# Low halves of q and k taken straight from PSUM, normalization on GpSimd, and new layouts for stored q, k and v

## The chip, the cores and the metric

The kernel runs on one core of a Trainium2 chip. The metric is the device time of one execution in microseconds, as the median of several runs. The engines are named as in the profile: PE (TensorE), DVE (VectorE), ACT (ScalarE), POOL (GpSimd) and SP (SyncE, whose queue issues every DMA of this kernel).

## The reference

The input x has 16 sequences of 512 rows with 128 features. Each row is normalized once (`_layernorm`), and two branches read the result:

```python
mu = jnp.mean(x, axis=-1, keepdims=True); var = jnp.var(x, axis=-1, keepdims=True)
xn = (x - mu) / jnp.sqrt(var + 1e-05) * ln_g + ln_b          # a second time, in the attention branch
q, k, v = xn @ Wq + bq, xn @ Wk + bk, xn @ Wv + bv            # 16 heads of 8 features
content = jnp.einsum('bihd,bjhd->bhij', q + u_bias, k)
pos = _relative_shift(jnp.einsum('bihd,jhd->bhij', q + v_bias, p))   # p = pe @ Wp
attn = softmax((content + pos) * scale); out = (attn @ v) @ Wo + bo
```

The other branch is a feed-forward net with weights of +1 and -1: `[x, -x] @ k0` (512 wide), relu, `@ k1` (512), relu, `@ k2` (128), with three scale factors. The output is the sum of x and both branches.

## The kernel before

The program has two stages. The first one prepares, batch by batch (b = 0 to 15), everything that attention reads, and computes the feed-forward net beside it. The second one is attention, head by head.

**Halves.** TensorE is fast with f16 operands, so a 32-bit value t is given as two f16 values, hi = f16(t) and lo = f16(t - hi), and products of halves are added. So q + u, q + v, k and the positions p each exist as a hi and a lo half. A power of two as a scale (`q_mul`, `k_mul`, found in `powers` at run time) keeps them within f16's range; `e_scale` undoes it at the exponential.

**The first stage.** `norm` (L308) computes mean and variance on DVE (L318, L319), a refined inverse root by a chain of 8-element operations (L325 to L333), and then writes xn in place with four 128x128 operations (L335). `transposed2` (L505) transposes xn on PE and writes its halves for the feed-forward net, and `with_bias` (L518) writes x2T, the input of the projections. `project_q` (L543) multiplies with `wq_d`; ACT reads the product twice with scale and bias (`scaled`, L522, line L528), once for q + u and once for q + v, into 32-bit tiles in SBUF; `halves_to` (L501) then casts the tile to hi on ACT (L502) and subtracts on POOL for lo (L503). `project_k` (L563) does the same once, through `stored` (L533). `project_v` copies v with ACT. All are stored to DRAM scratch tensors with DMAs: `qu_scr` (a zero-interleaved pair of columns for each value, four parts), `k_scr` (four parts, each half twice), `v_scr` and, after all batches, `qv_scr` (`quads_stored`, L599).

The feed-forward net runs between: for each batch four products of layer 0 (2 matmuls each, L640), four of layer 1 (8 matmuls each, L640), and the last layer (32 matmuls, L674). A product of layer 0 or 1 is split in halves by ACT and DVE (`split`, L617 and L618) before the next layer reads it. Its result is added to the residual, which POOL prepares (`ffn_residual`, L662) and DVE finishes (`ffn_out`, L688).

**PSUM.** Six tiles `s_t` of one bank, `t_t` and `a_t` are in use. The feed-forward products rotate over four banks (`F_BANKS`, L190), and everything else that goes through `psw` (L235) over three.

**Order.** In the first stage the program's text gives priorities (the list `queue` and the function `more`, L749, put the items of the attention preparation between the feed-forward products; `SPAN` = 12.3 batches is how far they are spread) and a scheduler decides the order on each engine. An engine works through its instructions in order; so does SP's queue, where a DMA that waits holds those behind it. In attention the order of PE, DVE and ACT is written out by hand (`STEPS`, L41), and SP and POOL are left to the scheduler.

**Attention.** A unit is four rows of queries of all 16 batches for one head; there are 512 units. `scores` (L785) adds the products of k and the two position windows in PSUM (L797, L813, L826), DVE finds maxima (L840, L845, L854), PE subtracts them (L859), ACT exponentiates (L869), PE multiplies with v (L887). At the second unit of each group of eight, `load_queries` (L210) issues the 12 DMAs of the next group's queries, into the one of two tiles that was used before; once a head, `load_head` (L196) issues the next head's k, windows and v. Once a head as well, `divided` (L939) loads sums and their reciprocals, multiplies them on POOL (L946) and stores them (L947).

Of the kernel before, what the change touches and what calls it, by code (L numbers as in the profile page):

```python
# [9 lines left out]
F32 = mybir.dt.float32  # L10
F32R = mybir.dt.float32r
F16 = mybir.dt.float16
# [3 lines left out]
AF = mybir.ActivationFunctionType  # L16
# [71 lines left out]
def rel_attention_and_binary_ffn(  # L88
# [47 lines left out]
    def scr(name, shape, dt):  # L136
# [3 lines left out]

    qu_scr = scr("qu_scr", [4, DH * H, B, S, 2], F16)
    qv_scr = scr("qv_scr", [4, DH * H, 5, NL, NC, UL, B], F16)
    k_scr = scr("k_scr", [4, DH * H, B, S], F16)
    p_scr = scr("p_scr", [4, DH * H, 2, WIN + 4], F16)
    pd_scr = scr("pd_scr", [4, DH * H, 2, 2, WIND + 1], F16)
    v_scr = scr("v_scr", [P, H, B, NC * VW], F32)

# [3 lines left out]
    res_scr = scr("res_scr", [B, S, D], F32)  # L151
    Q_PARTS, K_PARTS = ((0, 2), (1, 3)), ((0, 1), (2, 3))

# [26 lines left out]

    s_t = [
        [ps.tile([P, 2, NC, 4, B], F32, tag=f"s_{n}_{m}", name=f"s_{n}_{m}") for m in range(2)]
        for n in range(3)
    ]
    t_t = ps.tile([P, 4, 2, P], BF16, tag="t", name="t_t")
# [3 lines left out]
    p_banks.append(t_t.rearrange("p n f i -> p (n f i)").bitcast(F32))  # L189
    F_BANKS = (3, 4, 5, 6)  # L190
    t_bank = p_banks[6].rearrange("p (g i) -> p g i", g=2)
# [4 lines left out]
    def load_head(h):  # L196
        m = h % 2
        src = p_scr.rearrange("t (d h) s j -> (t d) h s j", h=H)[:, h]
        src_d = pd_scr.rearrange("t (d h) s n j -> (t d) h s n j", h=H)[:, h]
        for n in range(4):  # L200
            rows_n = slice(32 * n, 32 * n + 32)
            nc.sync.dma_start(
                k_t[m][rows_n], k_scr.rearrange("t (d h) b j -> (t d) h b j", h=H)[:, h, n::4, :]
            )
            nc.sync.dma_start(win[m][rows_n], src[:, :, 3 - n : 3 - n + WIN])
            r, side = n // 2, n % 2
            nc.sync.dma_start(win_d[m][rows_n], src_d[:, side, :, 1 - r : 1 - r + WIND])
        nc.sync.dma_start(v_t[m], v_scr[:, h].rearrange("p b f -> p (b f)"))

    def load_queries(h, l):  # L210
        m = l % 2
        qv = qv_scr.rearrange("t (d h) r l a u b -> (t d) h r l (a u b)", h=H)[:, h, :, l]
        qu = qu_scr.rearrange("t (d h) b i m -> (t d) h b (i m)", h=H)[:, h]
        for n in range(4):
            rows_n = slice(32 * n, 32 * n + 32)
            nc.sync.dma_start(
                qc_t[m][rows_n, :, n // 2].rearrange("p g i m -> p g (i m)"),
                qu[:, n::4, 2 * l * P : 2 * (l + 1) * P],
            )
            nc.sync.dma_start(  # L220
                qp_t[m][rows_n, :, n].rearrange("p s a u b -> p s (a u b)"), qv[:, n : n + 2]
            )
            r, side = n // 2, n % 2
            nc.sync.dma_start(
                qd_t[m][rows_n, :, r].rearrange("p t a u b -> p t (a u b)"),
                qv[:, r + side : r + side + 3 : 2],
            )


    with ExitStack() as pre:  # L230
# [19 lines left out]
        xn_all = {}  # L250
        XB = 4
        RB = 3
# [55 lines left out]
        def norm(b):  # L308
# [25 lines left out]
            for c in range(NC):  # L334
                nc.vector.tensor_scalar(  # L335
                    xn[:, c, :], xn[:, c, :], st1[:, b, c, 0:1], r[:, 1, c : c + 1], ALU.subtract, ALU.mult
                )
# [66 lines left out]
        pw = sts("pw", [P, 2])  # L404
        k_mul = pw[:, 1:2]
        q_mul = sts("q_mul", [P, 1])
        b_cols = sts("b_cols", [P, 3])
# [14 lines left out]
        def powers():  # L422
# [24 lines left out]
            nc.vector.tensor_scalar(e_scale, e_scale, 2.0 ** -26, None, ALU.mult)  # L447
            for n in range(2):
# [6 lines left out]
        def positions():  # L455
            pp = psw("pp")
            nc.tensor.matmul(pp, lhsT=wp_d, rhs=pe_sb, start=True, stop=True)
            p32 = work.tile([P, S], F32, tag="t32", name="p32", bufs=2)
            nc.scalar.activation(p32, pp, AF.Identity, scale=k_mul)
            halves_to(p32, *[t[:, PAD : PAD + S] for t in p_half])  # L460

        def windows():
            for n in range(2):
                for part in K_PARTS[n]:
# [20 lines left out]
        def clear():  # L485
            for t in v_b:
                nc.gpsimd.memset(t, 1.0)
            for t in p_half:
                nc.gpsimd.memset(t, 0.0)
            for ts in qu_b:  # L490
                for t in ts:
                    nc.gpsimd.memset(t, 0.0)

# [6 lines left out]

        def halves_to(src, hi, lo):  # L501
            nc.scalar.copy(hi, src)  # L502
            return nc.gpsimd.tensor_tensor(lo, src, hi, ALU.subtract)  # L503

# [16 lines left out]

        def scaled(b, n, src, dst):  # L522

            mul = k_mul if n == 2 else q_mul
            if n < 2:
                src = src.rearrange("p (a l m) -> p l a m", a=NC, l=NL)
                dst = dst.rearrange("p (l a m) -> p l a m", l=NL, a=NC)
            nc.scalar.activation(dst, src, AF.Identity, bias=b_cols[:, n : n + 1], scale=mul)  # L528

        def t32(b, n):  # L530
            return work.tile([P, S], F32, tag="t32", name=f"t32_{b}_{n}", bufs=2)

        def stored(b, t, dst, parts):  # L533
            hv = [work.tile([P, S], F16, tag=f"hv{m}", name=f"hv{m}_{b}", bufs=2) for m in range(2)]
            last = halves_to(t, *hv)
            for m in range(2):
                for part in parts[m]:
                    nc.sync.dma_start(dst[part, :, b, :], hv[m])
            return last

        two = {}

        def project_q(b):  # L543
            pq = psw(f"pq_{b}")
            nc.tensor.matmul(pq, lhsT=wq_d, rhs=x2T[b], start=True, stop=True)
            n = b % 2

            if n == 0:
                two[0] = work.tile([P, S, 2], F32, tag="two", name=f"two_{b}", bufs=1)
            tu = t32(b, 0)  # L550
            scaled(b, 0, pq, tu)
            scaled(b, 1, pq, two[0][:, :, n])
            halves_to(tu, *[t[:, :, n] for t in qu_b[n]])
# [3 lines left out]
            if n == 1:  # L557
                halves_to(
                    two[0].rearrange("p (q r) n -> p r q n", r=4),
                    *[q[:, :, :, b - 1 : b + 1] for q in qv_all],  # L560
                )

        def project_k(b):  # L563
            pk = psw(f"pk_{b}")
            nc.tensor.matmul(pk, lhsT=wk_d, rhs=x2T[b], start=True, stop=True)
            t = t32(b, 2)
            scaled(b, 2, pk, t)
            last = stored(b, t, k_scr, K_PARTS)
            with tc.issue_after(last.ins):
                clear_queries(b)  # L570

        def project_v(b):
# [13 lines left out]
            )  # L586
            nc.sync.dma_start(v_scr[:, :, b, :], vb.rearrange("p h c w -> p h (c w)"))

# [69 lines left out]
        def ffn_residual(b):  # L658
            res = last_res if b == LAST else spare[:, 4 + b % (RB + 1)]
            rows_of = res.rearrange("p (c d) -> p c d", c=NC)  # L660
            nc.sync.dma_start(rows_of, x[b].rearrange("(c p) d -> p c d", p=P))
            nc.gpsimd.tensor_tensor(rows_of, rows_of, bo_sb.unsqueeze(1).to_broadcast([P, NC, D]), ALU.add)  # L662
            acts[b, 3] = res
# [70 lines left out]
        for b in range(B):  # L734
            queue.append(lambda b=b: project_q(b))
            if b + 3 < B:
# [410 lines left out]
```

## Time and profile before

| what | value |
|---|---|
| median of 3 runs | 1378.01 us (1374.29 to 1380.7) |
| profiled execution, its own time | 1373.51 us |
| its span, first to last instruction | 1371.7 us |
| granted TensorE clock, mean | 0.985 |
| busy: PE, DVE, ACT, POOL | 1295.0, 1137.7, 832.6, 130.8 us |
| first attention matmul | 266.5 us after the span's start |
| DMA bytes | 160.22 MB, mean 117 GB/s |

How to read it: all times are microseconds unless ns is written. A row of a table of stretches gives busy time of the engines in a stretch of the span, with the number of instructions; a row of a timeline gives the start, the duration, the engine, the line of the program, the operation, and output <- input, with the idle time before it and what ended that in brackets. A row of waits gives who waited for whom: us in total, times, longest.

### The profile page before, as it was taken

What the parts mean: (1) busy time and instruction counts of PE and PEld (TensorE: products, weight loads), DVE (VectorE), ACT (ScalarE), POOL (GpSimd) and SP (SyncE); (2) the same over time, 40 slices, a digit from 0 to 9 for tenths busy, and PEclk for the clock granted to TensorE, in tenths of its full rate; (3) what the DMA queues carried; (4) which work ended last, traced back from release to release, by engine and by line L of the source; (5) the groups of instructions that cost most, each with busy time, mean ns of one, the idle gap of its engine ahead of it and who ended that gap; (6) DMA issues with size and microseconds to landing.
All of it is one profiled execution on the core that took longest, in us unless ns stands there. A gap on an engine that the chain in (4) does not pass through costs nothing. (4 is left out here: it accounts for less than half of the span.)

```text
span 1371.7 us, 55178 instructions
## 1 busy us (share of the span) xinstructions
PE 1295.0 (94%) x23061; PEld 970.3 (71%) x23061; DVE 1137.7 (83%) x2723; ACT 832.6 (61%) x1456; POOL 130.8 (10%) x115
## 2 busy tenths in 40 slices
PE   4988889999999999999999999999999999999966
PEld 2555555577778777777877877778777777777744
DVE  8988754688888888888888888888888888888846
ACT  4566668466666666666666666666666666566630
POOL 4333345010000000000000000000000000000011
PEclk9999999999999999999999999999999999999988
DMA  4587869873232333333333323333333253323288
GB/s 117 171 222 192 191 171 257 242 220 92 76 99 74 94 79 95 95 86 86 93 89 83 94 74 97 83 93 84 95 80 99 75 128 84 95 74 88 68 146 190
DMA packets 243606, 160.22 MB, mean 117 GB/s; under 512 B 79510, under 2 KB 227100, under 8 KB 243356
## 3 DMA queue, kind: packets, MB, share of 16 engines
q1 hardware_dynamic: 243356, 156.69, 43.5%
q8 instruction: 181, 2.97, 0.9%
q14 instruction: 69, 0.57, 0.1%
HBM read 96.34 MB, written 59.48 MB: 114 GB/s over the span
## 5 line engine op out<-in xcount | busy, mean ns | idle before, releaser
L869 ACT ACTIVATE e<-s,e_scale 128x512 f32<-128x512 f32 x1024 | 623.7, 690 | 218.2 <-PE s L859 218.1
L845 DVE TENSOR_TENSOR m<-s,m 128x256 bf16<-128x256 f32 x1024 | 431.6, 422 | 112.9 <-PE s L826 77.6
L797 PE MATMUL s<-q,k 128*128 128x64 f16 x8192 | 406.7, 193 | 2.1 <-issue 1.0
L859 PE MATMUL s<-ident_b,nm 128*128 128x256 bf16 x2048 | 383.8, 275 | 7.3 <-DVE nm L854 7.3
L797 PEld LDWEIGHTS <-k 128*128 128x128 f16 x8192 | 358.5, 98 | 23.6 <-issue 2.8
L840 DVE TENSOR_REDUCE m<-s 128x256 bf16<-128x512 f32 x512 | 348.2, 680 | 1.0 <-ACT e L869 0.6
L813 PE MATMUL s<-q,win 128*128 128x128 f16 (+1 forms) x4096 | 342.8, 206 | 0.1
L887 PE MATMUL a_t<-e,v 128*9 128x256 f32 x4032 | 266.0, 381 | 0.6 <-ACT e L869 0.6
L813 PEld LDWEIGHTS <-win 128*128 128x128 f16 x4096 | 231.4, 98 | 0.3 <-issue 0.3
L826 PE MATMUL s<-q,win_d 128*128 128x64 f16 x2048 | 227.7, 193 | 0.0
L854 DVE TENSOR_REDUCE nm<-t_t 128x2 bf16<-128x256 bf16 x512 | 214.7, 419 | 7.1 <-PE t_t L850 2.9
L859 PEld LDWEIGHTS <-nm 128*128 128x128 bf16 x2048 | 131.0, 98 | 117.8 <-DVE m L845 99.0
L896 ACT COPY av<-a_t 128x256 f32<-128x256 f32 x126 | 46.9, 372 | 186.2 <-PE a_t L887 161.2
L887 PEld LDWEIGHTS a_t<-e,v 128*9 128x9 f32 x4032 | 86.4, 90 | 81.2 <-issue 1.6
L850 PE MATMUL t_t<-ident_b,m 128*128 128x128 bf16 x1024 | 141.3, 220 | 1.4 <-DVE m L845 1.3
L826 PEld LDWEIGHTS <-win_d 128*128 128x128 f16 x2048 | 129.8, 98 | 0.0
L946 POOL TENSOR_TENSOR raw<-raw,rden 128x512 f32<-128x512 f32 x15 | 19.1, 1273 | 992.3 <-DMA rden<-rden_scr 992.3
L640 PEld LDWEIGHTS <-e 128*128 128x128 f16 x512 | 49.6, 98 | 59.7 <-issue 12.6
L850 PEld LDWEIGHTS <-m 128*128 128x128 bf16 x1024 | 80.9, 98 | 11.3 <-DVE m L845 4.9
L618 DVE SCALAR_TENSOR_TENSOR h2l<-s,h2h 128x512 f16<-128x512 f32 x45 | 30.9, 686 | 37.6 <-ACT h2h L617 37.4
L640 PE MATMUL s<-h1l,e 128*128 128x512 f16 x180 | 47.2, 379 | 0.5 <-DVE h1l L618 0.4
L640 PE MATMUL s<-h1h,e 128*128 128x512 f16 x180 | 47.2, 384 | 0.3 <-DVE h1l L618 0.2
(176 smaller groups left out, 888.3 us busy)
## 6 DMA issues: line engine op xcount, KB each, us to landing
q<-qv_scr SPq DMA_DIRECT2D x512, 64.0 KB
q<-qu_scr SPq DMA_DIRECT2D x256, 64.0 KB
qu_scr<-k SPq DMA_DIRECT2D x32, 256.0 KB
k_scr<-hv SPq DMA_DIRECT2D x64, 128.0 KB
qu_scr<-win SPq DMA_DIRECT2D x32, 256.0 KB
qv_scr<-e SPq DMA_DIRECT2D x16, 512.0 KB
k<-k_scr SPq DMA_DIRECT2D x64, 128.0 KB
win<-p_scr SPq DMA_DIRECT2D x64, 79.5 KB
```

The source lines that it names most:

```text
L640: nc.tensor.matmul(ph, lhsT=w[:, t, f * P : (f + 1) * P], rhs=h[t][m], start=(m == 0 and t == 0), stop=(m == 1 and t == n - 1),)
L797: nc.tensor.matmul(sp[:, c % 2, :, :, 4 * g : 4 * g + 4].rearrange("p a r (n m) -> p n (a r) m", m=2), lhsT=kt[:, g, c * P : (c + 1) * P], ...
L813: nc.tensor.matmul(blocks[:, x0 : x0 + (NC + 1) * (len(cs) - 1) + 1 : NC + 1], lhsT=win[h % 2][:, side, y0 : y0 + P], rhs=qp[:, side, :, c ...
L826: nc.tensor.matmul(blocks[:, x0 : x0 + NC + 2 : NC + 1, 2 * t : 2 * t + 2], lhsT=win_d[h % 2][:, t, UP_OFF - 4 * u : WIND - 4 * u], rhs=qd ...
L840: nc.vector.tensor_reduce(st["m"], flat(st["ps"][0]).rearrange("p c x -> p x c"), AX.X, ALU.max)
L845: nc.vector.tensor_tensor(st["m"], flat(st["ps"][1])[:, c], st["m"], ALU.max)
L850: nc.tensor.transpose(st["pt"][:, f, :], st["m"][:, f * P : (f + 1) * P], ident_b)
L854: nc.vector.tensor_reduce(st["nm"], st["pt"], AX.X, ALU.max, negate=True)
L859: nc.tensor.matmul(flat(st["ps"][half])[:, :, f * P : (f + 1) * P], lhsT=st["nm"][:, f : f + 1].to_broadcast([P, P]), rhs=ident_b.unsqueez ...
L869: nc.scalar.activation(st["eT"][:, :, cs, :, i0 : i0 + 4].rearrange("p b c a r -> p (c a) b r"), st["ps"][half].rearrange("p c a r b -> p ...
L887: nc.tensor.matmul(bank[32 * r : 32 * r + VW, g], lhsT=v_t[h % 2][:, v0 : v0 + VW], rhs=pair["eT"][:, b, c], start=(c == 0 and (g == 0 or ...
L896: nc.scalar.copy(pair[half][:, g], bank[:, g])
```

## The change

- `halves_to` takes the product in PSUM itself: ACT writes hi with the bias, and DVE (no longer POOL) computes lo = (product + bias) - hi in one operation. The scale is no longer applied there; instead the weights `wp_d`, `wq_d` and `wk_d` are multiplied by `q_mul` or `k_mul` once, in `powers`. The 32-bit tiles in SBUF and `scaled` are gone.
- q is projected for two batches at once, into a pair of banks of its own. The two batches of a pair now stand side by side in `qu_scr`, in place of one batch and zeros, so it is half as large. `load_queries` loads both columns and then clears the other batch's column with a POOL memset, four for each group.
- `k_scr` has two parts instead of four, and `load_head` loads each twice. `v_scr` has batch ahead of head: the store is one piece for each partition, and the load of a head takes 16 pieces.
- The four 128x128 operations of `norm` move from DVE to POOL.
- The feed-forward net has three banks instead of four, the rest of `psw` two instead of three. Six x tiles are kept instead of four. `clear_queries` moves from behind the k halves to behind the residual. The clearing of the staging tiles of q + u goes.

```diff
-    qu_scr = scr("qu_scr", [4, DH * H, B, S, 2], F16)
+    qu_scr = scr("qu_scr", [4, DH * H, B // 2, S, 2], F16)
-    k_scr = scr("k_scr", [4, DH * H, B, S], F16)
+    k_scr = scr("k_scr", [2, DH * H, B, S], F16)
-    v_scr = scr("v_scr", [P, H, B, NC * VW], F32)
+    v_scr = scr("v_scr", [P, B, H, NC * VW], F32)
-    Q_PARTS, K_PARTS = ((0, 2), (1, 3)), ((0, 1), (2, 3))
+    Q_PARTS, P_PARTS, K_PARTS = ((0, 3), (1, 2)), ((0, 2), (1, 3)), ((0,), (1,))
...
-    F_BANKS = (3, 4, 5, 6)
+    F_BANKS = (4, 5, 6)
+    q_banks = s_two[0].rearrange("p m c a r b -> p m (c a r b)")
...
-            nc.sync.dma_start(
-                k_t[m][rows_n], k_scr.rearrange("t (d h) b j -> (t d) h b j", h=H)[:, h, n::4, :]
-            )
+            for x in range(2):
+                nc.sync.dma_start(
+                    k_t[m][32 * n + 16 * x : 32 * n + 16 * x + 16],
+                    k_scr.rearrange("t (d h) b j -> (t d) h b j", h=H)[:, h, n::4, :],
+                )
...
-                qu[:, n::4, 2 * l * P : 2 * (l + 1) * P],
-            )
+                qu[:, n // 2 :: 2, 2 * l * P : 2 * (l + 1) * P],
+            )
+            nc.gpsimd.memset(qc_t[m][rows_n, :, n // 2, :, 1 - n % 2], 0.0)
...
-        def psw(name, banks=(0, 1, 2)):
+        def psw(name, banks=(2, 3)):
...
-        XB = 4
+        XB = 6
...
             for c in range(NC):
-                nc.vector.tensor_scalar(
+                nc.gpsimd.tensor_scalar(
                     xn[:, c, :], xn[:, c, :], st1[:, b, c, 0:1], r[:, 1, c : c + 1], ALU.subtract, ALU.mult
                 )
...
-            nc.vector.tensor_scalar(q_mul, pw[:, 0:1], scale, None, ALU.mult)
+            for t, mul in ((wp_d, k_mul), (wq_d, q_mul), (wk_d, k_mul)):
+                nc.vector.tensor_scalar(t, t, mul, None, ALU.mult)
...
-        def halves_to(src, hi, lo):
-            nc.scalar.copy(hi, src)
-            return nc.gpsimd.tensor_tensor(lo, src, hi, ALU.subtract)
+        def halves_to(src, n, hi, lo):
+            nc.scalar.activation(hi, src, AF.Identity, bias=b_cols[:, n : n + 1])
+            for r in range(4) if len(src.shape) == 4 else [slice(None)]:
+                nc.vector.scalar_tensor_tensor(
+                    lo[:, r], src[:, r], b_cols[:, n : n + 1], hi[:, r], ALU.add, ALU.subtract
+                )
...
         def project_q(b):
+            for n in range(2):
+                nc.tensor.matmul(
+                    q_banks[:, n],
+                    lhsT=wq_d,
+                    rhs=x2T[b + n].rearrange("p (a l m) -> p l a m", a=NC, l=NL),
+                    start=True,
+                    stop=True,
+                )
+            qu = qu_b[b // 2 % 2]
+            halves_to(q_banks.rearrange("p n j -> p j n"), 0, *qu)
             for m in range(2):
                 for part in Q_PARTS[m]:
-                    nc.sync.dma_start(qu_scr[part, :, b], qu_b[n][m])
+                    nc.sync.dma_start(qu_scr[part, :, b // 2], qu[m])
+            halves_to(
+                q_banks.rearrange("p n (q r) -> p r q n", r=4), 1, *[q[:, :, :, b : b + 2] for q in qv_all]
+            )
...
-            nc.sync.dma_start(v_scr[:, :, b, :], vb.rearrange("p h c w -> p h (c w)"))
+            nc.sync.dma_start(v_scr[:, b], vb.rearrange("p h c w -> p h (c w)"))
...
         for b in range(B):
-            queue.append(lambda b=b: project_q(b))
+            if b % 2:
+                queue.append(lambda b=b: project_q(b - 1))
```

More of the change, by code (lines that the diff above doesn't have):

```diff
@@ L179, in rel_attention_and_binary_ffn @@
     a_t = ps.tile([P, 2, 2 * P], F32, tag="a", name="a_t")
[L181 to L184, printed above, removed]
+    s_two = [ps.tile([P, 2, 2, NC, 4, B], F32, tag=f"s_{n}", name=f"s_{n}") for n in range(3)]
+    s_t = [[t[:, m] for m in range(2)] for t in s_two]
     t_t = ps.tile([P, 4, 2, P], BF16, tag="t", name="t_t")
@@ L207, in load_head @@
             nc.sync.dma_start(win_d[m][rows_n], src_d[:, side, :, 1 - r : 1 - r + WIND])
-        nc.sync.dma_start(v_t[m], v_scr[:, h].rearrange("p b f -> p (b f)"))
+        nc.sync.dma_start(v_t[m].rearrange("p (b f) -> p b f", b=B), v_scr[:, :, h])
     def load_queries(h, l):
@@ L404, in rel_attention_and_binary_ffn @@
         pw = sts("pw", [P, 2])
-        k_mul = pw[:, 1:2]
-        q_mul = sts("q_mul", [P, 1])
+        q_mul, k_mul = pw[:, 0:1], pw[:, 1:2]
         b_cols = sts("b_cols", [P, 3])
@@ L444, in powers @@
             nc.vector.tensor_scalar(pw, pw, 2.0 ** 13, None, ALU.mult)
-            nc.vector.tensor_scalar(q_mul, pw[:, 0:1], scale, None, ALU.mult)
+            for t, mul in ((wp_d, k_mul), (wq_d, q_mul), (wk_d, k_mul)):
+                nc.vector.tensor_scalar(t, t, mul, None, ALU.mult)
             nc.vector.tensor_tensor(e_scale, bmax[:, 0:1], bmax[:, 1:2], ALU.mult)
-            nc.vector.tensor_scalar(e_scale, e_scale, 2.0 ** -26, None, ALU.mult)
+            nc.vector.tensor_scalar(e_scale, e_scale, 2.0 ** -26 * scale, None, ALU.mult)
             for n in range(2):
@@ L457, in positions @@
             nc.tensor.matmul(pp, lhsT=wp_d, rhs=pe_sb, start=True, stop=True)
-            p32 = work.tile([P, S], F32, tag="t32", name="p32", bufs=2)
-            nc.scalar.activation(p32, pp, AF.Identity, scale=k_mul)
-            halves_to(p32, *[t[:, PAD : PAD + S] for t in p_half])
+            hi, lo = [t[:, PAD : PAD + S] for t in p_half]
+            nc.scalar.copy(hi, pp)
+            nc.vector.tensor_tensor(lo, pp, hi, ALU.subtract)
         def windows():
             for n in range(2):
-                for part in K_PARTS[n]:
+                for part in P_PARTS[n]:
                     for side, x0, d0 in ((0, PAD, PAD + S - P + 2), (1, 0, PAD - P + 1)):
@@ L489, in clear @@
                 nc.gpsimd.memset(t, 0.0)
-            for ts in qu_b:
-                for t in ts:
-                    nc.gpsimd.memset(t, 0.0)
         def clear_queries(b):
@@ L520, in with_bias @@
             nc.scalar.activation(x2T[b], flipped.pop(b), AF.Identity, bias=b_c, scale=g_c)
[L522 to L541, printed above, removed]
-        def project_q(b):
[L544 to L553, printed above, removed]
+        def project_q(b):
+            for n in range(2):
[8 more added lines that the diff above has]
+            halves_to(q_banks.rearrange("p n j -> p j n"), 0, *qu)
             for m in range(2):
                 for part in Q_PARTS[m]:
-                    nc.sync.dma_start(qu_scr[part, :, b], qu_b[n][m])
[L557 to L560, printed above, removed]
-                )
+                    nc.sync.dma_start(qu_scr[part, :, b // 2], qu[m])
+            halves_to(
+                q_banks.rearrange("p n (q r) -> p r q n", r=4), 1, *[q[:, :, :, b : b + 2] for q in qv_all]
+            )
         def project_k(b):
@@ L565, in project_k @@
             nc.tensor.matmul(pk, lhsT=wk_d, rhs=x2T[b], start=True, stop=True)
[L566 to L570, printed above, removed]
+            hv = [work.tile([P, S], F16, tag=f"hv{m}", name=f"hv{m}_{b}", bufs=3) for m in range(2)]
+            halves_to(pk, 2, *hv)
+            for m in range(2):
+                for part in K_PARTS[m]:
+                    nc.sync.dma_start(k_scr[part, :, b, :], hv[m])
         def project_v(b):
@@ L661, in ffn_residual @@
             nc.sync.dma_start(rows_of, x[b].rearrange("(c p) d -> p c d", p=P))
-            nc.gpsimd.tensor_tensor(rows_of, rows_of, bo_sb.unsqueeze(1).to_broadcast([P, NC, D]), ALU.add)
+            last = nc.gpsimd.tensor_tensor(
+                rows_of, rows_of, bo_sb.unsqueeze(1).to_broadcast([P, NC, D]), ALU.add
+            )
+            with tc.issue_after(last.ins):
+                clear_queries(b)
             acts[b, 3] = res
```

## Prediction

> **What bounds the kernel now.** I read the page's first rows, then a table of stretches, to see which stage has anything to give.
>
> ```profile
> span 1371.7 us, 55178 instructions
> ...
> PE 1295.0 (94%) x23061; PEld 970.3 (71%) x23061; DVE 1137.7 (83%) x2723; ACT 832.6 (61%) x1456; POOL 130.8 (10%) x115
> ```
>
> ```profile
> 0.00:40.00 40.00, 20.40 (x103) 10.97 (x103) 33.14 (x115) 15.92 (x33) 15.45 (x27) 0.96 0.37 101
> 40.00:180.00 140.00, 121.79 (x707) 70.83 (x707) 118.09 (x385) 90.83 (x162) 54.11 (x44) 0.95 0.77 201
> 180.00:266.00 86.00, 84.72 (x554) 49.81 (x554) 43.78 (x84) 61.15 (x103) 29.61 (x24) 0.98 0.84 231
> 300.00:1300.00 1000.00, 991.65 (x20492) 779.41 (x20490) 876.36 (x2019) 628.49 (x1098) 17.83 (x14) 1.00 0.33 88
> ```
>
> The columns are the stretch, then busy time of PE, weight loads, DVE, ACT and POOL, the granted clock, the DMA share and GB/s. From 300 us on (attention) PE is busy 99%, at full clock, and the change leaves PE's work there alone. So the gain must come from the 266 us before it, where the first attention matmul starts at 266.5 us. Busy PE is not PE at its peak, so I count its work: the timeline starts four 512-column f16 matmuls (L640) every 0.86 us, four 128-column ones (L674) every 0.22, a projection (L545, L565) every 0.86, four transposes in 0.43. Up to attention the program has 616 of L640 (16 batches x 8 of layer 0, 15 x 32 of layer 1 and 8 of the last), 132 us, 480 of L674, 26, q and k 28, v 14, transposes 7, the rest 3: about 211 us. Of 266 us PE loses 55; counted by stretch 24 before 40 us, 27 between 40 and 180, and 3 after 180. The middle stretch is where to look; its waits (engine, line and what it waited for: us, times, longest):
>
> ```profile
> ACT h2h L617 <- PE s L640: 17.0, 7, 4.6
> PE s L640 <- DVE h2l L618: 14.8, 7, 3.9
> DVE h2l L618 <- ACT h2h L617: 10.8, 8, 3.2
> ```
>
> PE waits for DVE to write the low half h2l, at the turn from one batch to the next. Nine such gaps over 0.7 us add up to 20 us; the other 7 are the stretches at half clock (0.95 mean). The longest gap, in three timelines (PE, DVE, POOL), shows why DVE is late:
>
> ```profile
> 119.51 0.59 PE L640 MATMUL t_t<-sums,w_sb 128*128 128x512 f16 x2
> 124.03 1.01 PE L640 MATMUL s<-sums,w_sb 128*128 128x512 f16 x2 [3.92 <-DVE h2l L618]
> ```
>
> ```profile
> 116.46 1.51 DVE L330 TENSOR_TENSOR step<-var,root 128x8 f32<-128x8 f32 x1
> 118.00 1.20 DVE L331 TENSOR_TENSOR step<-step,root 128x8 f32<-128x8 f32 x1
> 119.23 1.54 DVE L332 TENSOR_SCALAR step<-step 128x8 f32<-128x8 f32 x1
> ...
> 121.87 0.85 DVE L335 TENSOR_SCALAR xn<-xn,st,root 128x128 f32<-128x128 f32 x3
> ...
> 123.28 0.69 DVE L618 SCALAR_TENSOR_TENSOR h2l<-s,h2h 128x512 f16<-128x512 f32 x1
> ```
>
> ```profile
> 115.03 2.91 POOL L503 TENSOR_TENSOR e<-two,e 128x1024 f16<-128x1024 f32 x1
> 117.91 1.26 POOL L662 TENSOR_TENSOR sums<-sums,bo_sb 128x512 f32<-128x512 f32 x1
> 119.14 1.15 POOL L503 TENSOR_TENSOR hv<-t,hv 128x512 f16<-128x512 f32 x1
> ```
>
> Three 8-element operations, whose median is 0.17 us, take 1.2 to 1.5, and each ends when a POOL instruction ends. DVE is held while POOL works, and PE's h2l stands behind these and behind L335.
>
> **The change, part by part.**
>
> ACT loses the scaled copies and casts of q and k (L528 36.3 us, L502 30.8). It gains sixteen 128x1024 activations and sixteen of 512: 1.15 (the 1024-element cast) and 0.62 us, 28 in all. ACT gives back 38 us; it is 65% busy in the middle, so this shortens only the 0.6 us links of the chain. Taken alone: 0.
>
> POOL loses L503 (62.8 us) and four staging memsets (3.8), and gains 64 normalizations of 128x128. Between the copies of that size (0.29) and the strided ones (0.47) I take 0.35: 22 us, with 19 and 30 as ends. POOL falls from 99 us before 266 to about 55.
>
> DVE loses L335 (24.9 us) and gains low halves from PSUM. k: 16 x 0.69 (L618's row). q+u: eight of 1024, 0.69 plus another 0.46, 1.15 each. q+v: 32 of 256, between 0.34 (128, L688) and 0.69 (512), 0.46 each. With three weight scalings 36.5 us, so +11.6. Against that, means over medians of the held rows (L332, L685, L325, L330, L331, L326, L333, L335, L339) come to 38 us of instruction time, some of it overlapping; I count 25 of wall time. If every POOL instruction holds DVE alike, 55/99 of it stays and 11 go; if only the two-input ones do, 20/83 stays and 19 go. I take 15. So DVE's total is about level. What changes is the place: in 40 to 180 it loses 21 (L335) and 11 of holding and gains 63% of the low halves, 22: 118 becomes 108, 77% busy, and the norm chain ahead of h2l is the part that shrinks.
>
> PE, middle stretch: per gap, 1.4 us of L335 and one or two POOL holds of about 1.2 go. The nine gaps hold 20 us; I take 10 off, and 4 of the 7 lost to the half clock, which appears where PE pauses: -14. Ends: 0 (low halves take the place of L335 in DVE's queue) and -24.
>
> [...] The granted clock fell to 0.95 between 40 and 180 us and is 1.00 in attention. [...]
>
> [...] POOL's two-input rows take 1.16 to 1.27 us for 512 columns where DVE takes 0.69. [...]
>
> Start, up to 40 us. PE waits 2.9 us at 14.8 to 17.5 for an operation behind L332, held 3.33 us by the memsets of L492, which go: -3. The first norm moves to POOL, 4 x 0.35 and 0.6 of copies in between: +1. Six x tiles instead of four let DVE's new order take norms of batches 3 to 6 before the projection scales, some 3 us each, which may stand before h2l: 0 to +9, I take +2 (most find DVE waiting). Net 0, ends -3 and +8.
>
> From 180 us: PE loses 3 there. FFN has three PSUM banks, not four, and transposes, k and v two, not three, now released by DVE too. A bank is freed about 1.35 us after its last matmul (0.6 ACT, 0.68 DVE); between two uses of a bank lie two others, 0.86 us in layer 0, with 1.8 us of L674 to put between. I take +1 for the whole stage; ends 0 and +40 (next part).
>
> DMA. qu_scr and k_scr stores halve (25.2 to 12.6 MB), against a share of 0.77 to 0.84: nothing waits on it but the hand-over to attention, where the last query load lands at about 261 us, 5 us early. v stores become one piece for each partition, and v loads 2048 pieces of 144 B. Such a store takes 1.9 to 4.0 us of DMA time (0.30 MB at 164 us), against 1.5 for the present load.
>
> Attention: each query load gains four memsets on POOL behind its DMAs, about 0.5 us each (128x512 is 0.52), and head loads four more issues on SP (0.45 each).
>
> ```profile
> 449.12 0.62 SPq L943 DMA_DIRECT2D rden<-rden_scr  x1
> ...
> 455.50 0.34 SPq L947 DMA_DIRECT2D head_scr<-raw  x1
> ```
>
> This is SP's tightest place, once a head: ten of twelve query loads queue behind a store that waits for POOL. The last is issued at 460.7, its packets end by 461, and it is needed when the group before ends, at 465.2: 4 us of slack. In the new order v is issued some 7 us earlier, before rden_scr, so this wait should shorten. The last memset follows the tenth of twelve loads, so it ends about with the twelfth. In POOL's order L946 stands before these memsets and waits for what SP has already issued. Taken: 0; ends -3 and +4.
>
> Sum: -14 + 0 + 1 + 0 = -13 us against the profiled execution's 1373.5 us, 1360.5. That execution lies 4.5 us below the median of the runs, 1378.0, so I forecast **1365 us**.
>
> **Rivals.** (1) Nothing to speak of: DVE's new low halves wait for ACT where L335 stood. For it: DVE's total stays level. Against: the holds are POOL's. 0 to -6: about 1375. (2) Larger: most of the middle loss goes and the clock stays up, -25: 1353. For it: nearly all gaps have the same cause. (3) Slower, by the FFN banks: the third and fourth layer-0 products wait for ACT and DVE. For it: DVE at 77% may keep a bank 2.5 us more; 16 batches x 2.5 = 40, less 13, is 1405. It decides from 20/16 = 1.25 us of wait a batch. Against: the new order puts L674 between them. (4) Slower, by late query loads: if v's 2048 pieces took 12 us, past the 7 + 4 us of cover, each further us costs 15. Against: 2 to 4 us as stores. 1390.
>
> **How the numbers follow.** Forecast (-7 to -20) 0.47, larger 0.21, nothing 0.15, banks 0.13, queries 0.04. About 0.5%, 7 us, is what a measurement can tell from no change: faster is forecast and larger, 0.68; same 0.15; slower 0.17. The range goes from 1347 (two thirds of rival 2) to 1386 (the small half of rivals 3 and 4): about 0.85. The forecast's own is 1358 to 1371.
>
> **What would show it.** First attention matmul at about 253 us; L332's mean near 0.3 us; PE's waits for h2l halved between 40 and 180; mean unit in attention still 2.05 us. Wrong if PE waits there on its banks (L623 on DVE or ACT inside layer 0), if the start passes 45 us, or if attention matmuls wait for POOL.

## The result, and the profile after

The changed kernel takes 1839.41 us (median of 4 runs, 1838.38 to 1840.64), beside 1379.36 us (1374.29 to 1381.16) for the kernel before: a ratio of 1.334, 95% interval 1.331 to 1.338. The forecast was 1365 us.

The page of the kernel after, its span and its engines:

```profile
span 1838.2 us, 55145 instructions
...
PE 1459.6 (79%) x23061; PEld 988.2 (54%) x23061; DVE 1186.4 (65%) x2718; ACT 884.5 (48%) x1399; POOL 285.6 (16%) x390
```

The number of matmuls is the same, 23061. The span is 466.5 us longer: PE is busy 164.6 us more (1459.6 - 1295.0) and idle 301.9 us more. The matmuls themselves are no slower (the groups shown below have 193 and 192 ns, 275 and 273 ns); there is more busy time because a matmul that follows a pause does not overlap with the one before (the eight L785 at 540.12 us start 0.03 us apart and last 0.19 us each, so an overlap of 0.16 us is missing at a pause). The table of stretches of the kernel after says where (columns as before: PE, weight loads, DVE, ACT, POOL, granted clock, DMA share, GB/s):

```profile
0.00:40.00 40.00, 18.97 (x86) 9.25 (x87) 29.43 (x128) 14.02 (x29) 24.63 (x42) 1.00 0.42 114
40.00:180.00 140.00, 128.06 (x766) 71.36 (x766) 111.18 (x357) 78.84 (x133) 53.53 (x67) 0.98 0.45 144
180.00:266.00 86.00, 79.82 (x489) 42.74 (x488) 48.89 (x88) 45.54 (x74) 10.51 (x14) 1.00 0.61 193
300.00:1300.00 1000.00, 789.46 (x14174) 553.63 (x14173) 640.92 (x1400) 488.01 (x761) 127.83 (x182) 1.00 0.24 61
```

In the middle of the first stage PE gets 128.06 us of work in place of 121.79, the way that was forecast. The loss is all in attention, the stage that the prediction had set at nothing: at full clock PE gets through 14174 matmuls in 1000 us, not 20492. The first attention matmul starts at 262.4 us (before 266.5), the last product of q and k at 1786.4 (1316.4): 1523.9 us in place of 1049.9. No engine is near full there, so something waits. The waits of the kernel after, over the span, attention's part:

```profile
ACT e L857 <- PE s L847: 531.3, 641, 3.4
...
PE s L847 <- ACT e L857: 174.2, 258, 1.7
PE s L785 <- DVE m L828: 106.9, 254, 0.8
```

The last two are new. L847 puts the row maxima into PSUM ahead of the exponentials (L859 before), L785 is the product of q and k (L797 before). In the kernel before these groups on its page have 7.3 and 2.1 us of idle time before them, for other reasons:

```profile
L797 PE MATMUL s<-q,k 128*128 128x64 f16 x8192 | 406.7, 193 | 2.1 <-issue 1.0
L859 PE MATMUL s<-ident_b,nm 128*128 128x256 bf16 x2048 | 383.8, 275 | 7.3 <-DVE nm L854 7.3
```

On the page of the kernel after they have 132.2 and 188.6:

```profile
L847 PE MATMUL s<-ident_b,nm 128*128 128x256 bf16 x2048 | 392.3, 273 | 188.6 <-ACT e L857 174.2
L785 PE MATMUL s<-q,k 128*128 128x64 f16 x8192 | 405.3, 192 | 132.2 <-DVE m L828 106.9
```

A stretch of PE's timeline in the kernel after shows one such wait:

```profile
536.33 0.39 PE L847 MATMUL s<-ident_b,nm 128*128 128x256 bf16 x2
536.56 0.27 PE L838 MATMUL t_t<-ident_b,m 128*128 128x128 bf16 x2
537.50 0.38 PE L847 MATMUL s<-ident_b,nm 128*128 128x256 bf16 x2 [0.67 <-ACT e L857]
537.72 0.40 PE L785 MATMUL s<-q,k 128*128 128x64 f16 x8
```

The L847 at 536.33 belongs to one half of a unit, the one at 537.50 to the other half, and it waits for ACT's exponential. The two halves lie in different banks. What the change did to them is in two lines of it that the prediction's list of parts does not have:

```diff
-    s_t = [
-        [ps.tile([P, 2, NC, 4, B], F32, tag=f"s_{n}_{m}", name=f"s_{n}_{m}") for m in range(2)]
-        for n in range(3)
-    ]
+    s_two = [ps.tile([P, 2, 2, NC, 4, B], F32, tag=f"s_{n}", name=f"s_{n}") for n in range(3)]
+    s_t = [[t[:, m] for m in range(2)] for t in s_two]
```

Six PSUM tiles of one bank become three of two banks, so that q of two batches can be read as one operand. The two halves of every unit, and neighbouring banks of the first stage, are then slices of one tile.

### The profile page after: what moved, and what is told of

It reads as the page before. It is cut to its first block, busy times and chain, and to the rows that moved or that the text cites. A ratio compares the mean times of both kernels' runs of the same rounds, so it can differ in the third digit from the quotient of the medians.

```text
span 1838.2 us, 55145 instructions
## 1 busy us (share of the span) xinstructions
PE 1459.6 (79%) x23061; PEld 988.2 (54%) x23061; DVE 1186.4 (65%) x2718; ACT 884.5 (48%) x1399; POOL 285.6 (16%) x390
## 5 line engine op out<-in xcount | busy, mean ns | idle before, releaser
L857 ACT ACTIVATE e<-s,e_scale 128x512 f32<-128x512 f32 x1024 | 702.4, 688 | 531.4 <-PE s L847 531.3
L847 PE MATMUL s<-ident_b,nm 128*128 128x256 bf16 x2048 | 392.3, 273 | 188.6 <-ACT e L857 174.2
L785 PE MATMUL s<-q,k 128*128 128x64 f16 x8192 | 405.3, 192 | 132.2 <-DVE m L828 106.9
L785 PEld LDWEIGHTS <-k 128*128 128x128 f16 x8192 | 354.0, 97 | 240.4 <-issue 204.3
L847 PEld LDWEIGHTS <-nm 128*128 128x128 bf16 x2048 | 161.5, 97 | 352.7 <-issue 235.4
L223 POOL MEMSET q<- 32x512 f16 x256 | 171.5, 670 | 1022.8 <-DMA q<-qu_scr 1022.3
L339 POOL TENSOR_SCALAR xn<-xn,st,root 128x128 f32<-128x128 f32 x64 | 50.4, 799 | 58.3 <-DVE root L337 19.6
```

Of the source, the lines that this page charges most:

```text
L223: nc.gpsimd.memset(qc_t[m][rows_n, :, n // 2, :, 1 - n % 2], 0.0)
L339: nc.gpsimd.tensor_scalar(xn[:, c, :], xn[:, c, :], st1[:, b, c, 0:1], r[:, 1, c : c + 1], ALU.subtract, ALU.mult)
L785: nc.tensor.matmul(sp[:, c % 2, :, :, 4 * g : 4 * g + 4].rearrange("p a r (n m) -> p n (a r) m", m=2), lhsT=kt[:, g, c * P : (c + 1) * P], ...
L847: nc.tensor.matmul(flat(st["ps"][half])[:, :, f * P : (f + 1) * P], lhsT=st["nm"][:, f : f + 1].to_broadcast([P, P]), rhs=ident_b.unsqueez ...
L857: nc.scalar.activation(st["eT"][:, :, cs, :, i0 : i0 + 4].rearrange("p b c a r -> p (c a) b r"), st["ps"][half].rearrange("p c a r b -> p ...
```

## The experiments

**Theory A** is that the shared tile makes the waits. Against it stood **theory B**, that what the change adds beside attention (the clearing of q on GpSimd, the small pieces of v, the further transfers) slows it, and **theory C**, that both are needed. The recorded expectations count attention in pairs of units, so "4.1 us a unit" there is twice the 2.05 of the prediction.

**1. The shared tiles alone, in the kernel before.** The edit is the diff just shown and nothing else.

> The kernel before, with one edit alone: the two halves of each score unit are slices of one two-bank PSUM tile, as in the change. Theory A (the shared tile makes PE wait between the halves: scores of the second half for DVE's maximum L828 of the first, the row-maximum matmul L847 of the second half for ACT's exponential of the first): the whole loss comes with this edit; attention takes 5.9 us a unit in place of 4.1, 1810 to 1850 us in all. Theory B (what slows attention is on the load side: the memsets of q on GpSimd, the 144-byte pieces of v, four more transfers a head): nothing of that is in this kernel, 1370 to 1385 us. Theory C (both are needed): between, near 1600.

1847.83 us in one run (before on the same chip: 1374.42, median of 7 runs). Attention takes 1515.2 us. The same two waits appear; the waits of this kernel:

```profile
ACT e L867 <- PE s L857: 532.1, 641, 3.4
...
PE s L857 <- ACT e L867: 174.2, 258, 1.7
PE s L795 <- DVE m L838: 107.9, 255, 1.5
```

174.2 and 107.9 us, beside 174.2 and 106.9 in the changed kernel. One grouping of banks makes a loss as large as the whole: 465 us of it in attention, 13 in the first stage (first attention matmul at 279.3 us). Theories B and C fall as explanations of it. That does not say that the rest of the change is harmless, which the next run asks.

**2. The changed kernel, shared tiles in the first stage only.**

```diff
-    s_two = [ps.tile([P, 2, 2, NC, 4, B], F32, tag=f"s_{n}", name=f"s_{n}") for n in range(3)]
+    ps_1 = tc.tile_pool(name="ps_1", bufs=1, space=bass.MemoryType.PSUM)
+    ps_pre = ps_1.__enter__()
+    s_two = [ps_pre.tile([P, 2, 2, NC, 4, B], F32, tag=f"s_{n}", name=f"s_{n}") for n in range(3)]
...
+    ps_1.__exit__(None, None, None)
+    ps_2 = ctx.enter_context(tc.tile_pool(name="ps_2", bufs=1, space=bass.MemoryType.PSUM))
+    s_t = [
+        [ps_2.tile([P, 2, NC, 4, B], F32, tag=f"s_{n}_{m}", name=f"s_{n}_{m}") for m in range(2)]
+        for n in range(3)
+    ]
     big_end = ExitStack()
```

> The changed kernel with the shared tiles kept for the first stage only: their PSUM pool is closed ahead of attention, and another with six one-bank tiles, as before, takes its place. Theory A: attention is back at 4.1 us a unit; first attention matmul near 262 us as in the changed kernel, 4 us earlier than before, so 1370 to 1376 us; the closing of the pool may cost one wait of a few us at the turn. Theory B: still 1800 to 1840. Theory C: near 1378 also, so this run alone does not tell A from C.

1464.22 us (1463.39 to 1465.04), ratio 1.065 (1.063 to 1.067): 375 us come back, 90 stay. So there is a second loss. Attention takes 1134.3 us, 84 more than before, and the first attention matmul comes at 272.4 us, 6 later. Once a head there is a pause. DVE in that kernel, its instructions on both sides of one:

```profile
543.06 0.88 DVE L841 TENSOR_TENSOR m<-s,m 128x256 bf16<-128x256 f32 x2 [0.31 <-PE s L822]
543.86 0.68 DVE L836 TENSOR_REDUCE m<-s 128x256 bf16<-128x512 f32 x1
550.30 0.25 DVE L925 RECIPROCAL den<-den 128x16 f32<-128x16 f32 x1 [5.76 <-DMA den<-av]
```

The same wait in the kernel before, where it is 0.63 us:

```profile
463.17 0.25 DVE L929 RECIPROCAL den<-den 128x16 f32<-128x16 f32 x1 [0.63 <-DMA den<-av]
```

`den` is a small transfer whose reciprocal stands at a fixed place in DVE's written order, with the next maxima behind it. On SP it comes behind the store of `raw`, which waits for POOL. SP's rows in the new kernel between the two:

```profile
536.15 0.34 SPq L943 DMA_DIRECT2D head_scr<-raw  x1
536.53 0.43 SPq L206 DMA_DIRECT2D k<-k_scr  x1
537.01 2.46 SPq L210 DMA_DIRECT2D win<-p_scr  x1
...
540.04 0.57 SPq L213 DMA_DIRECT2D v<-v_scr  x1
...
548.40 0.60 SPq L917 DMA_DIRECT2D den<-av  x1
```

Sixteen transfers stand between the store and `den`: four of the next head's loads and 12 of queries. In the kernel before there are nine (the store at 455.50, `den` at 461.23). In the changed kernel itself there are ten at every head, so this second loss is not in it: SP's order is left to the scheduler, and it came out differently for run 2. DVE's pause stops PE for 5.32 us in this place, and the granted clock falls to 0.96 over attention, where it was 1.00.

**3. The changed kernel, one pair of banks shared throughout.**

```diff
-    s_two = [ps.tile([P, 2, 2, NC, 4, B], F32, tag=f"s_{n}", name=f"s_{n}") for n in range(3)]
-    s_t = [[t[:, m] for m in range(2)] for t in s_two]
+    s_two = [ps.tile([P, 2, 2, NC, 4, B], F32, tag="s_0", name="s_0")]
+    s_t = [[s_two[0][:, m] for m in range(2)]] + [
+        [ps.tile([P, 2, NC, 4, B], F32, tag=f"s_{n}_{m}", name=f"s_{n}_{m}") for m in range(2)]
+        for n in (1, 2)
+    ]
```

> The changed kernel with only s_0 a two-bank tile (the one that the query projections need) and s_1, s_2 as four one-bank tiles. Theory A: one unit in three has the extra waits: a third of 465 us, 155, on 1374, so 1520 to 1540 us; less (down to 1450) where the neighbouring units' work fills the pause. Theory B: 1800 to 1840.

1582.69 us (one run), more than expected. Attention takes 1291.1 us, 241 more than before: one shared unit in three costs half of the 474 us of three, not a third, so the neighbours do not fill its pause. The unexpected part is the first stage: its last feed-forward product before attention starts at 240 us, where it was 266.3 before and 262.2 in the changed kernel. Only the tiles of the feed-forward and projection banks differ from the changed kernel there.

**4. As run 2, normalizing products back on DVE.** 
```diff
-                nc.gpsimd.tensor_scalar(
+                nc.vector.tensor_scalar(
                     xn[:, c, :], xn[:, c, :], st1[:, b, c, 0:1], r[:, 1, c : c + 1], ALU.subtract, ALU.mult
                 )
```

> As the kernel with the shared tiles in the first stage only, and the normalizing products back on DVE. The prediction's step (normalizing on DVE stands ahead of h2l; moving it is worth most of 14 us between 40 and 180 us): 8 to 14 us slower than with it on GpSimd, 1380 to 1388 us. If the 0.80 us that GpSimd was measured to take for one 128x128 product, and PE's 10 us wait for it at the start, eat the gain: the same within 4 us, or faster, 1366 to 1374.

1453.89 us (1448.33 to 1456.22), 10 us faster than run 2, and not 8 to 14 slower: normalizing on GpSimd is no gain here.

**5. One shared pair in the first stage, one-bank tiles otherwise.** Runs 2 and 3 led to **theory D**: the 90 us are two losses, waits that the shared tiles make on the first stage's banks (some 30 us) and SP's order at the head's turn (some 84). **Theory E**: they come from closing the pool or from the turn between stages.

```diff
-    s_two = [ps_pre.tile([P, 2, 2, NC, 4, B], F32, tag=f"s_{n}", name=f"s_{n}") for n in range(3)]
-    s_t = [[t[:, m] for m in range(2)] for t in s_two]
+    s_two = [ps_pre.tile([P, 2, 2, NC, 4, B], F32, tag="s_0", name="s_0")]
+    s_t = [[s_two[0][:, m] for m in range(2)]] + [
+        [ps_pre.tile([P, 2, NC, 4, B], F32, tag=f"s_{n}_{m}", name=f"s_{n}_{m}") for m in range(2)]
+        for n in (1, 2)
+    ]
```

> First stage: only s_0 a two-bank tile, the four FFN and projection banks one tile each; attention: six one-bank tiles. Two theories on the 90 us that stayed with the shared tiles confined to the first stage. Theory D (two separate losses: shared tiles also hold the FFN banks in the first stage, some 30 us; and once a head DVE waits 5 to 6 us at the reciprocal L920 for the small load den, which SP issues behind 16 transfers after the store of raw, where before there were 9): only the first goes here; first attention matmul near 240 us as with one pair kept throughout, attention still some 1134 us, 1430 to 1440 us in all. Theory E (the 90 us come from the closing of the pool or from the order at the turn): unchanged near 1464.

1428.87 us (1425.52 to 1432.61), ratio 1.041 (1.038 to 1.043). The first attention matmul is at 240.2 us, 32 us earlier than in run 2, and attention stays at 1135.5, as theory D has it. The stretches of this kernel:

```profile
180.00:240.00 60.00, 59.53 (x396) 33.97 (x395) 39.49 (x73) 35.23 (x58) 7.07 (x10) 1.00 0.71 221
300.00:1300.00 1000.00, 940.47 (x18892) 741.84 (x18890) 808.65 (x1856) 581.22 (x1014) 165.75 (x235) 0.96 0.31 81
```

Three feed-forward banks are enough: PE loses 0.5 us of the 60 up to 240. The second row still has the pauses.

**6. Head loads one query group earlier.** 
```diff
-                    if nl % NL == 0:
-                        load_head(nl // NL)
+                    if nl % NL == NL - 1 and nl // NL + 1 < H:
+                        load_head(nl // NL + 1)
```

> As the kernel with one pair in the first stage, and the next head's k, windows and v loaded one query group earlier, so that 9 transfers, not 16, stand between the store of raw and den on SP. Theory D: the once-a-head pause is gone, attention back at 1050 us; 240 + 1050 + 56 = 1346, so 1340 to 1355 us. Theory E, or a pause that is made by GpSimd's clearing of q in place of SP's order: 1420 to 1440.

1452.74 us (1452.02 to 1459.47): slower than run 5, with nine transfers between the store and `den`. The edit was at fault: v is loaded too, into the buffer of the head before, whose last products come later in the program, so these products take the next head's v and wait for it. This kernel's waits between 500 and 1000 us:

```profile
PEld a_t L886 <- DMA v<-v_scr: 38.6, 6, 7.1
PE a_t L886 <- DMA v<-v_scr: 37.6, 6, 6.9
```

So the run's time does not decide on theory D, though DVE's waits for `den` in attention, 69.6 us at 14 heads in run 5, are gone from its trace.

**7. As run 6, normalizing products on DVE,** by the edit of run 4.

> As the kernel with the early head loads, with the normalizing products back on DVE. The prediction's step (products on DVE hold h2l): 8 to 14 us slower, 1354 to 1366. What the pair of kernels with shared tiles in the first stage showed (DVE 10 us faster): 1336 to 1342. With the banks apart the term may be nothing: within 3 us.

1456.36 us (1455.13 to 1458.7); it has the same wait for v, and the same change in what is computed, so its total tells little. In the first stage, which v does not touch, the last product before attention comes at 239.1 us, beside 239.7.

**8. As run 5, k stored four times and loaded in four pieces, as before the change.**

```diff
-    k_scr = scr("k_scr", [2, DH * H, B, S], F16)
+    k_scr = scr("k_scr", [4, DH * H, B, S], F16)
...
-    Q_PARTS, P_PARTS, K_PARTS = ((0, 3), (1, 2)), ((0, 2), (1, 3)), ((0,), (1,))
+    Q_PARTS, P_PARTS, K_PARTS = ((0, 3), (1, 2)), ((0, 2), (1, 3)), ((0, 1), (2, 3))
...
-            for x in range(2):
-                nc.sync.dma_start(
-                    k_t[m][32 * n + 16 * x : 32 * n + 16 * x + 16],
-                    k_scr.rearrange("t (d h) b j -> (t d) h b j", h=H)[:, h, n::4, :],
-                )
+            nc.sync.dma_start(
+                k_t[m][rows_n], k_scr.rearrange("t (d h) b j -> (t d) h b j", h=H)[:, h, n::4, :]
+            )
```

> As the kernel with one pair in the first stage, with k stored four times and loaded in four pieces a head, as before the change, so that alone these stores and loads are undone. Theory D: SP's order has 9 transfers between the store of raw and den again, the pause goes: 1340 to 1355. If the pause comes from the clearing of q or the 144-byte pieces of v: 1420 to 1440.

1359.53 us (1357.2 to 1361.23), ratio 0.990 (0.988 to 0.992). Attention takes 1060.8 us, with the clearing of q and the small pieces of v unchanged. The scheduler now puts nine transfers between the store and `den` at 13 of the 14 heads; at the other there are 15, and DVE waits 4.5 us for `den` there.

**9. As run 5, all the change's pieces kept, only k and the windows loaded one query group earlier, v where it was.** `load_v` is the last line of `load_head`, taken out of it.

```diff
-                    if nl % NL == 0:
-                        load_head(nl // NL)
+                    if nl % NL == NL - 1 and nl // NL + 1 < H:
+                        load_head(nl // NL + 1)
+                    if nl % NL == 0:
+                        load_v(nl // NL)
```

> As the kernel with one pair in the first stage (k still in eight pieces a head), with the next head's k and windows, not v, loaded one query group earlier: 9 transfers, not 16, between the store of raw and den. Theory D (SP's order makes the pause, not the size or number of the pieces): the pause goes with all the pieces kept, 1345 to 1362 us. If k's 16-partition pieces cost by themselves: 1420 to 1435.

1348.78 us (1345.82 to 1351.71), ratio 0.981 (0.980 to 0.983). Attention is back at 1052.1 us with k in eight pieces, so SP's order made the pause: nine transfers stand there again at all 14 heads. The stretches of this kernel:

```profile
40.00:180.00 140.00, 134.39 (x844) 78.56 (x844) 115.44 (x357) 84.19 (x146) 56.04 (x70) 1.00 0.48 158
180.00:240.00 60.00, 59.53 (x396) 33.98 (x394) 39.49 (x73) 35.18 (x58) 7.30 (x10) 1.00 0.70 221
300.00:1290.00 990.00, 981.50 (x20285) 771.24 (x20283) 865.42 (x1991) 622.82 (x1089) 177.28 (x252) 1.00 0.34 88
```

Every part of the change that the prediction listed is in this kernel, and it beats the one before by 26 us, all of it in the first stage (first attention matmul at 240.1 us, 26.4 earlier).

**10. As run 8, normalizing products on DVE,** by the edit of run 4.

> As the kernel with k whole, with the normalizing products back on DVE. By the prediction's step 8 to 14 us slower, 1368 to 1374. By the two kernels with early head loads, whose last first-stage products came at 239.7 and 239.1 us: no difference, 1356 to 1363.

1355.61 us (1355.24 to 1357.28), 3.9 us faster than run 8. DVE is busy 127.17 us of the 140 between 40 and 180, and PE's waits for it do not come back.

**11. Run 8 and run 9 together,** by both edits.

> k whole and the next head's k and windows one query group earlier. Attention still has some 11 us more than before in the kernel with k whole, in pauses of 4 us at DVE's reciprocal L926 of den; if SP's order there is to blame too, they go: 1347 to 1352 us. If not: 1356 to 1363.

1348.24 us (1346.17 to 1351.09), ratio 0.981 (0.980 to 0.982); attention 1050.1 us. With the order mended, k in four pieces or eight makes no difference (1348.24 and 1348.78).

**12. The kernel before, with the low halves L503 on VectorE.** What are the 26 us of the first stage? **Theory F**: GpSimd's two-input operations hold DVE. **Theory G**: the amount of DVE's work decides.

```diff
-            return nc.gpsimd.tensor_tensor(lo, src, hi, ALU.subtract)
+            return nc.vector.tensor_tensor(lo, src, hi, ALU.subtract)
```

> The kernel before, with one edit alone: the low halves L503 are taken off GpSimd and computed on VectorE from the same staging tiles. It asks what the 26 us of the first stage come from. Theory F (GpSimd's two-input operations hold DVE, and PE waits behind): the holds of 1.2 to 1.5 us go although DVE gets some 32 us more work (33 of 512 at 0.66, eight of 1024 at 1.3); the first stage shortens by 5 to 20 us: 1355 to 1370. Theory G (DVE's amount of work sets the stage; the change gains because the low halves cost DVE nothing beyond what L335 did): 1378 to 1400.

1364.85 us (1362.05 to 1368.3), ratio 0.994 (0.991 to 0.997). DVE has 35.3 us of low halves more to do and the first attention matmul still comes 7.4 us earlier, at 259.1. Theory F holds, for 7 of the 26 us as a net. The net has a loss at the start in it, where one L332 lies beside GpSimd's memsets for 9.87 us (3.33 in the kernel before):

```profile
13.29 9.87 DVE L332 TENSOR_SCALAR step<-step 128x8 f32<-128x8 f32 x1
23.19 0.17 DVE L333 TENSOR_TENSOR root<-root,step 128x8 f32<-128x8 f32 x1
23.27 0.68 DVE L621 SCALAR_TENSOR_TENSOR sums<-s,sums 128x512 f16<-128x512 f32 x1
```

PE waits 9.5 us for this L621 (2.9 before), and up to 40 us gets 14.81 us of work in place of 20.40; between 40 and 180 it gets 128.88 in place of 121.79. With that L332 left out, the means over medians of the rows that the prediction lists as held fall from 35 us in the kernel before to 13.

## Why the prediction was wrong

**The step that failed** is the one on attention: "the change leaves PE's work there alone", and then "Taken: 0; ends -3 and +4". The work did stay; the waits did not. That part priced loads and POOL's clearing. The PSUM tiles it did not price: the working counted banks ("FFN has three PSUM banks, not four") and not which of them were one tile. The price was 474 us on 1050 (262.4 to 1786.4 in place of 266.5 to 1316.4; a unit 2.98 us in place of 2.05): 281 of it in the two waits named by the profile, some 30 more idle before the same two lines, and the rest, about 165, in matmuls that no longer overlap. PE, DVE and ACT run attention's matmuls, maxima and exponentials in the same order in both traces; what differs is the waits that the instructions carry. Between 500 and 700 us each unit of the kernel after has one L847 that waits for ACT and one L785 that waits for DVE, and in the kernel before no L859 waits for ACT and no L797 for DVE. The two halves of a unit were meant to overlap on PE, DVE and ACT, and the two further waits stand in every unit.

The loads and the clearing, as far as they were priced, were not at fault: in run 9, with one-bank tiles and k and the windows loaded earlier, attention takes 2.2 us more than before, within the -3 and +4.

**Rivals.** None of the four had it. The slower ones named the right neighbourhoods with the wrong mechanism. Late query loads (1390) was close to the second loss: it watched the last query load, with 4 us of slack, where the transfer behind it, `den`, had none (DVE already waited 0.63 us for it). Its price, 15 us for each further us, was of the right kind: seven more transfers held DVE's maxima 4 to 7 us longer at 14 heads. The four more k loads, "0.45 each", were counted, but the order in which the scheduler would put them against the store of `raw` was not. In the changed kernel itself, with ten transfers there, DVE waits 4.4 us for `den` in all, and that behind attention. With 16 and without the first loss it costs 85.6 us (run 5 against before).

The clock is part of that. In the kernel before, DVE's maxima of successive units start 2.05 us apart on average; the pauses at the 14 heads of run 5 are 66 us above that in sum. The other 20 us lie right behind the pauses: at each head the granted clock is half for 3.4 or 6.8 us, 89 us in all, and a unit takes 3.1 us there. The first such place and the stretch behind it, in run 5:

```profile
373.70:380.50 6.80, 5.45 (x68) 4.88 (x68) 4.16 (x10) 2.70 (x4) 1.17 (x2) 0.50 0.26 69
380.50:445.00 64.50, 61.89 (x1280) 48.35 (x1277) 53.36 (x122) 38.63 (x68) 10.40 (x16) 1.00 0.31 81
```

Shorter gaps had half clock behind them too. In the kernel before, two gaps of 1.45 and 2.03 us, with a little work between them, are followed by 3.4 us at 0.51:

```profile
177.60:181.00 3.40, 0.87 (x4) 0.34 (x4) 2.74 (x8) 2.31 (x4) 0.00 (x0) 1.00 0.64 130
181.00:184.40 3.40, 3.40 (x32) 3.18 (x31) 1.96 (x4) 2.87 (x6) 1.27 (x1) 0.51 0.47 175
```

**FFN banks.** Forecast +1 with an end of +40. Three banks cost nothing (run 5: 0.5 us lost of 60), but shared tiles cost 32 us (run 2 against run 5) or 22 (the changed kernel against run 3): banks 4 and 5, of the feed-forward net, were one tile, and so were 2 and 3, of the transposes, k and v. No run parts the two pairs; PE's waits for ACT and DVE at the feed-forward line, up to 275 us, are 18.7 us in run 2 (L625) and 6.1 in run 5 (L628). In the changed kernel 180 to 266 us loses 6.2, where the kernel before loses 1.3.

**Middle of the first stage.** Forecast -14 with -24 as end, and -13 for the whole first stage; in the changed kernel the first stage gives 4.1 us, and with the banks apart 26.4 (run 9). The mechanism was half right. That POOL holds DVE was right. The groups of DVE's 8-element chain in the kernel before, up to 266 us:

```profile
L330 DVE TENSOR_TENSOR step<-var,root 128x8 f32<-128x8 f32 x16 | 6.4, 408 | 0.3
L331 DVE TENSOR_TENSOR step<-step,root 128x8 f32<-128x8 f32 x16 | 5.5, 351 | 0.3
L332 DVE TENSOR_SCALAR step<-step 128x8 f32<-128x8 f32 x16 | 9.9, 627 | 0.3
```

and the same three in run 9:

```profile
L341 DVE TENSOR_TENSOR step<-var,root 128x8 f32<-128x8 f32 x16 | 3.2, 198 | 0.2
L342 DVE TENSOR_TENSOR step<-step,root 128x8 f32<-128x8 f32 x16 | 3.0, 186 | 0.2
L343 DVE TENSOR_SCALAR step<-step 128x8 f32<-128x8 f32 x16 | 3.3, 205 | 0.2
```

Means over medians, summed over the lines that the prediction lists, fall from 38 us to 8.5 (7.8 of the 38 were L335's, which is no longer on DVE). But the move of L335 out of h2l's way was worth nothing: with the products back on DVE (runs 4 and 10) the kernel is 4 to 10 us faster, and PE's waits for h2l between 40 and 180 us stay small (2.8 us in run 10, 2.5 in run 8, 16.3 before). What run 12 does not cover, some 19 us of the 26, goes with the rest of the change (no 32-bit staging tiles, half of the stores, the x tiles and the bank numbers) and with what run 12 lost at its start; no run divides it.

**Start.** Forecast 0 with +8 as end. PE's first wait for the normalized x is 10.4 us in run 8, on GpSimd, and 8.4 in run 10, on DVE, so the move costs about 2. A GpSimd product was taken as 0.35 us and measured 0.80, 50 us in all in place of 22; POOL had the room.

**ACT.** Busy 803.4 us in run 8, where the kernel before has 832.6: 29 less, not 38. No run tests what that is worth alone.

## What to carry to other kernels

Where tiles are regrouped so that one operand can span them, read the changed program's list of waits in the stage that you believe untouched: a tile is also the unit by which waits are made, and here joining two banks of a pair that was meant to run overlapped added a third to the kernel's time. When a large loss is removed, read the new program's queues again: where a scheduler makes the order, the next tight place (here a small transfer, `den`, behind seven more on SP) can come with the repair itself. In a queue with a slow store at its head, count what stands between that store and the next transfer that an engine's written order depends on.

## What the runs showed of the hardware

A 128x128 product with two per-partition scalars takes 0.80 us on GpSimd, where DVE takes 0.34 (median of L335), and a clearing of 32x512 f16 with a stride of two takes 0.67:

```profile
L223 POOL MEMSET q<- 32x512 f16 x256 | 171.5, 670 | 1022.8 <-DMA q<-qu_scr 1022.3
```

GpSimd's hold on DVE depends on what GpSimd runs. Of DVE's L330, L331 and L333 (both inputs in SBUF) in the kernel before, 12 overlap one of GpSimd's two-input operations (L503, L662), and nine of them last 0.5 to 1.8 us in place of 0.17. In run 8, 25 of the same instructions overlap one of the normalizing products (one tensor input), and none lasts over 0.29 us (mean 0.17). Memsets, which read no tensor, ran beside the L332 of 9.87 us in run 12, which has one input.
